# Expert products: the passes with the crossed tokens of two chunks placed behind the other passes of both

## The chip, the core and the metric

The kernel runs on one core of a Trainium2 chip. The metric is the device time of one execution in microseconds (us). Times are medians of several executions; the profile is of one execution, with its own time. The engines are named as in the profile: PE (matmuls), PEld (the loading of PE's stationary operand), DVE (vector), ACT (scalar), POOL (GpSimd) and SP, which issues most DMAs.

## The reference, cut to what matters

There are 32 images of 64 x 1024. Each of two layers runs them through a chain of four small convolutions whose weights depend on a style vector, and then through a feed-forward part that is added to the input. The first feed-forward part has 64 experts of rank 16, of which each token takes 16; the second is one 1024 x 1024 product with 4-bit weights.

```python
def ffn0(x, A, B, Wr):                  # the part that the change touches
    scores = xf @ Wr.T                                   # 2048 tokens x 64 experts
    top_vals, top_idx = top_k(scores, 16)
    G = zeros.at[..., top_idx].set(softmax(top_vals))
    h = einsum('nd,krd->nkr', xf, A)                     # 2048 x (64 * 16)
    return einsum('nkr,kdr->nd', h * G[:, :, None], B) * 2.0

x = x + ffn0(cond0(x, style), A, B, Wr)
x = x + ffn1(cond1(x, style), qweight, scales, zeros, bias)
```

## The kernel before, in words

The images are taken in 16 pairs p, a pair being 128 tokens of 1024 features. There are three stages.

The first stage, `layer0(p)` with what is called around it, makes h. For each pair the loop that begins at line 899 computes the convolutions of later pairs (`begin`: the matmuls of lines 546, 551 and 459; `later`: line 571, called r after the tile that it writes, one call for each of the pair's two images; `weights`: line 480, tile f; `turn`: the transposes of line 621) and, between them, the products of this pair's tokens with the router and the A matrices. These have 64 + 1024 columns and are made in three chunks: c0 with 352 columns, c1 and c2 with 368 each. `layer0` is a generator that yields after each chunk; the loop runs the first chunk, then `later(k + 1, 0)`, the second chunk, then `later(k + 1, 1)` and `weights(k + 2)`, the third chunk, and then the transposes for the next pair.

A product of two fp32 numbers is made of three passes (limbs) in a faster number format. The tokens are split into a high part `th` and a rest `tl` (`split`, lines 589 to 593; the rest is scaled by ACT in line 597), and POOL makes the crossed tokens `td` as their difference in `crossed` (line 605, called at the end of a repetition, after `turn`). The weights are split in the same way into three limbs (`split_weights`, lines 287 to 299; the third limb, which the crossed tokens meet, is made by DVE in line 296 from the other two). The passes with `th` and `tl` add up in one PSUM bank and the passes with `td` in a second one. A pass is 8 matmuls, one for each 128 features. `joined` puts both banks together: ACT reads the first (line 680), DVE the second (line 681). After c0 DVE also finds the 16 best experts (`gates`, lines 685 to 703, with an exponential on ACT in line 698), and POOL multiplies h by the gates at the end (line 709), from where it is stored to `hgd` (line 723). The pairs 0 and 1 (`WHOLE`) are not split: they have one pass of full fp32 matmuls and no crossed tokens.

The second stage, `layer0b(p)`, multiplies h by the B matrices in two chunks of 512 columns, with the same three passes and again no split for the pairs 0 and 1. The rows of h are loaded (line 727) and turned for pair p + 1 (line 739, tile ht) ahead of the products of pair p (tile o). Its `joined` (lines 775 and 776) adds the rows of x, loaded in line 764 into a single region, and the sum is stored to `x1d` (line 798). During the first of these pairs DVE, ACT and POOL also split the B matrices (lines 143, 294, 295, 296) and, from pair 2 to 6, prepare the second layer's convolutions step by step (`factors`, for instance lines 193, 196, 207 and 210). The last pair takes its passes in another order: feature block outermost (`outer=True`).

The third stage, from about 691 us, makes the second layer (`layer1`); its products are written by its own code (line 819).

PSUM is shared out in pools of banks: `cps` has three, for r, the transposes and the c matmuls; `mps` has one, for f and g; `fps` has four, for the products. The buffers `rt` and `ru` of `rest` are single.

The instructions of each engine run in one order, which is fixed when the program is built. The order follows the source in the main, but not in every place: where the builder finds an instruction not yet ready, it can place a later one of the same engine ahead. The semaphore waits are set by it too.

The helper that writes the products is this:

```python
        if outer:
            ...
        else:
            for banks, cols in chunks:
                for l in limbs:
                    for k in range(NC):
                        go(k, l, banks, cols)
```

It is called with one chunk at a time (lines 715 and 795), so each chunk has its passes th, tl, td one after the other, directly followed by its `joined`.

Of the kernel before, what the change touches and what calls it, by code (L numbers as in the profile page):

```python
# [24 lines left out]
NC = L // P  # L25
H = 512
E = 64
R = 16
# [9 lines left out]
CHUNKS = ((0, 18), (18, 41), (41, 64))  # L38
# [23 lines left out]
def adaln_ffn_kernel(ctx: ExitStack, tc: tile.TileContext, t, out: bass.AP):  # L62
    nc = tc.nc
# [19 lines left out]
    def fpst(name):  # L83
        return fps.tile([P, H], F32, tag="fps", name=name)
# [47 lines left out]
    def tokens(tag, name, dt=F32R):  # L132

        return tok.tile([P, NC, P], dt, tag=tag, name=name)
# [464 lines left out]
    toks = {}  # L599
# [37 lines left out]

        return k ^ 1

    def products(chunks, key, ws, order, outer=False):  # L640


        limbs = range(len(toks[key]))

        def go(k, l, banks, cols):
            ps = banks[l == 2]
            w = ws[order(k)]
            if len(limbs) > 1:
                w = w[:, l]
            nc.tensor.matmul(  # L650
                ps,
                toks[key][l][:, k],
                w[:, cols],
                start=(k == 0 and l != 1),
                stop=(k == NC - 1 and l == min(2 * (l // 2) + 1, len(limbs) - 1)),
            )

        if outer:
            for k in range(NC):
                for banks, cols in chunks:  # L660
                    for l in limbs:
                        go(k, l, banks, cols)
        else:
            for banks, cols in chunks:
                for l in limbs:
                    for k in range(NC):
                        go(k, l, banks, cols)

    def layer0(p, ws):

        hs = wk.tile([P, AW], F32, tag="w4", name=f"hs{p}", bufs=3)
        key = f"x0_{p}"
        whole = p in WHOLE

        def joined(col, w, qd):
            dst = hs[:, col : col + w]
            if whole:
                nc.scalar.copy(dst, qd[0])
                return
            nc.scalar.activation(dst, qd[0], AF.Copy, scale=1.0 + 1.0 / RADIX)  # L680
            nc.vector.scalar_tensor_tensor(dst, qd[1], -1.0 / RADIX, dst, ALU.mult, ALU.add)  # L681

        ga = tiny.tile([P, E], F32, tag="ga", name=f"ga_{p}")

        def gates():
            s0 = hs[:, :E]
            m0 = tiny.tile([P, 8], F32, tag="m0", name=f"m0_{p}")
            m1 = tiny.tile([P, 8], F32, tag="m1", name=f"m1_{p}")
            s1 = tiny.tile([P, E], F32, tag="s1", name=f"s1_{p}")
            s2 = tiny.tile([P, E], F32, tag="s2", name=f"s2_{p}")  # L690
            nc.vector.max(m0, s0)
            nc.vector.match_replace(s1, m0, s0, LOW)
            nc.vector.max(m1, s1)
            nc.vector.match_replace(s2, m1, s1, LOW)
            nm = tiny.tile([P, 1], F32, tag="nm", name=f"nm_{p}")
            nc.vector.tensor_scalar_mul(nm, m0[:, 0:1], -1.0)
            ex = tiny.tile([P, E], F32, tag="ex", name=f"ex_{p}")
            nc.scalar.activation(ex, s0, AF.Exp, bias=nm)
            su = tiny.tile([P, 1], F32, tag="su", name=f"su_{p}")
            nc.vector.scalar_tensor_tensor(ga, s2, LOW, ex, ALU.is_equal, ALU.mult)  # L700
            nc.vector.reduce_sum(su, ga, axis=AX.X)
            nc.vector.reciprocal(su, su)
            nc.vector.tensor_scalar_mul(ga, ga, su)

        def gated(c):
            a, b = CHUNKS[c]
            v = hs[:, E + a * R : E + b * R].rearrange("p (e r) -> p e r", r=R)
            g = ga[:, a:b].unsqueeze(2).to_broadcast([P, b - a, R])
            nc.gpsimd.tensor_tensor(v, v, g, ALU.mult)  # L709

        col = 0
        for c, (a, b) in enumerate(CHUNKS):
            w = (b - a) * R + (E if c == 0 else 0)
            qd = [fpst(f"h{p}_{c}_{j}")[:, :w] for j in range(1 if whole else 2)]
            products([(qd, slice(col, col + w))], key, ws, at)
            joined(col, w, qd)
            if c == 0:
                gates()
            col += w
            yield  # L720
        for c in range(3):
            gated(c)
        nc.sync.dma_start(hgd[p], hs[:, E:])
# [30 lines left out]
    def layer0b(p, ws):  # L754

        whole = p in WHOLE
        key = f"h{p}"
        if whole:
            xres = tokens("tl", f"xres{p}", F32).rearrange("p a b -> p (a b)")
        elif p < NP - 1:  # L760
            xres = cv[:, O_Y + 2 * Y : O_Y + 2 * Y + L]
        else:
            xres = wk.tile([P, L], F32, tag="w4", name="xres", bufs=3)
        nc.sync.dma_start(xres, t["x"][p])
        x1 = wk.tile([P, L], F32, tag="w4", name=f"x1_{p}", bufs=3)
        x4 = x1.rearrange("p (f j) -> p j f", f=4)

        def banks(c):
            return [fpst(f"o{p}_{c}_{j}") for j in range(1 if whole else 2)]

        def joined(c, qd):
            cs = slice(c * H, (c + 1) * H)
            v = xres[:, cs]
            if not whole:
                nc.vector.scalar_tensor_tensor(v, qd[1], -SCALING / RADIX, v, ALU.mult, ALU.add)  # L775
            nc.vector.scalar_tensor_tensor(
                x4[:, c * P : (c + 1) * P],
                qd[0].rearrange("p (j f) -> p j f", f=4),
                SCALING if whole else SCALING * (1.0 + 1.0 / RADIX),
                v.rearrange("p (j f) -> p j f", f=4),  # L780
                ALU.mult,
                ALU.add,
            )

        cols = [slice(c * H, (c + 1) * H) for c in range(2)]
        if p == NP - 1:
            qds = [banks(c) for c in range(2)]
            products(list(zip(qds, cols)), key, ws, lambda k: k, outer=True)
            yield
            for c in range(2):  # L790
                joined(c, qds[c])
        else:
            for c in range(2):
                qd = banks(c)
                products([(qd, cols[c])], key, ws, lambda k: k)
                joined(c, qd)
                yield
        nc.sync.dma_start(x1d[p].rearrange("p f j -> p (f j)"), x1)
        v = x1.rearrange("p (f j) -> p j f", f=4)
        for s, js in enumerate((slice(0, 2), slice(L // 4 - 2, L // 4))):  # L800
            nc.gpsimd.tensor_copy(xg[:, p, s].rearrange("p (j f) -> p j f", f=4), v[:, js])
# [97 lines left out]
    for k in range(NP):  # L899
# [4 lines left out]
        if ahead:  # L904
            load(k + 3)
            for h in range(2):
                later(k + 1, h)
            weights(k + 2)
        main = layer0(k, araw if k in WHOLE else wa)
        next(main)  # L910
        if k == 0:
# [31 lines left out]
    for p in range(NP):  # L943
# [4 lines left out]
        if p == NP - 1:  # L948
            clear_y((2, 3))
            begin(NP + 1)  # L950
        main = layer0b(p, braw if p in WHOLE else wb)
        next(main)
        if p in WHOLE:
# [88 lines left out]
```

## Time and profile before

| what | value |
|---|---|
| median of three runs | 1026.52 us (1018.68, 1026.52, 1026.8) |
| profiled execution, its own time | 1025.0 us |
| span in the profile | 1023.2 us |
| mean granted clock of PE | 0.982 |
| PE busy | 958.0 us in 5046 instructions |
| DVE, POOL, ACT busy | 617.5, 462.6, 371.5 us |

The span runs from the first to the last instruction of the program; the execution's own time is 1.8 us longer. The profile's rows show the line of the source, the engine, the tiles written and read (out<-in), the shape, and the number of instructions. In a list of waits the three numbers are the sum in us, the number of waits and the longest one. In a timeline the first two numbers are start and length in us, and a bracket shows how long the engine had been idle and what ended that. An fp32 matmul appears as two records, one of a split pass as one. Since matmuls are pipelined, a record's length is larger than the step from one start to the next.

### The profile page before, as it was taken

The page shows a single profiled execution, that of the slowest core. Times are in us where ns is not written, and L with a number is a line of the kernel's source. Part 1 is how long each engine was busy: PE and PEld are TensorE (multiplying, and loading weights), DVE is VectorE, ACT ScalarE, POOL GpSimd, SP SyncE. Part 2 cuts the span into 40 slices and gives each one's busy share as a digit, 9 for nine tenths or more (in the row PEclk, how much of TensorE's full clock was granted, in tenths as well). Part 3 has the DMA queues.
Part 4 walks back from the last instruction along what each step waited for, and adds up shares of the span by engine and source line. Part 5 has one row for each costly group of instructions (what it writes and reads, how often), then busy time and mean ns, then how long its engine had stood idle before and what let it go on. Part 6 is the DMA issues. An engine that isn't in the chain of part 4 may idle for free.

```text
span 1023.2 us, 14297 instructions
## 1 busy us (share of the span) xinstructions
PE 958.0 (94%) x5046; PEld 842.8 (82%) x5046; DVE 617.5 (60%) x1153; ACT 371.5 (36%) x697; POOL 462.6 (45%) x748
## 2 busy tenths in 40 slices
PE   4789899999999999989889999999899999999997
PEld 4566689999999999885578887888899999999987
DVE  4586465555555555346874444476667776777654
ACT  4255344444444443323331111253333433433331
POOL 4375644444444444435822223225555545555544
PEclk9899899999999999999999999999999999999999
DMA  8323022222222222143333433243111221222111
GB/s 248 86 62 83 20 56 69 63 63 62 62 62 63 62 64 76 67 145 113 107 133 131 139 127 123 83 139 130 62 63 62 92 95 62 76 82 92 42 62 42
DMA packets 40823, 88.84 MB, mean 87 GB/s; under 512 B 13104, under 2 KB 21552, under 8 KB 40752
## 3 DMA queue, kind: packets, MB, share of 16 engines
q1 hardware_dynamic: 39792, 86.94, 26.9%
q10 hardware_dynamic: 960, 0.99, 0.3%
q8 instruction: 40, 0.66, 0.3%
q14 instruction: 31, 0.25, 0.1%
HBM read 62.74 MB, written 25.17 MB: 86 GB/s over the span
## 4 chain that ended last, share of the span: by engine, by line
PE 45%; DVE 4%; ACT 2%; issue 2%; POOL 2%; DMA 1%; POOLq 0%; SPq 0%; DVEq 0%; ACTq 0%
PE o L650 15%; PE q L819 12%; PE r L571 8%; PE f L480 4%; PE c L551 3%; PE h L650 1%; PE ht L739 1%; DVE h L143 1%; DMA cv<-in_x_dram 1%; ACT yt L548 1%; DVE sc L833 1%; PE c L546 1%; ACT wq L347 1%; DMA xb<-x1d 1%; POOL wb L294 0%
## 5 line engine op out<-in xcount | busy, mean ns | idle before, releaser
L571 PE MATMUL r<-cv 128*128 128x256 f32 (+1 forms) x768 | 178.5, 381 | 2.9 <-ACT rt L584 1.5
L571 PEld LDWEIGHTS r<-cv 128*128 128x128 f32 x768 | 142.7, 190 | 23.4 <-ACT rt L584 2.3
L584 ACT ACTIVATE rt<-r,cst,al 128x256 f32<-128x256 f32 x128 | 72.2, 564 | 181.0 <-PE r L571 143.4
L585 DVE TENSOR_TENSOR rs<-rt,ru 128x256 f32<-128x256 f32 x64 | 43.6, 681 | 98.9 <-ACT rt L584 54.8
L480 PEld LDWEIGHTS f<-gs,w1b 128*128 128x128 f32 x576 | 87.1, 193 | 3.1 <-ACT gs L468 1.1
L480 PE MATMUL f<-gs,w1b 128*128 128x192 f32 (+1 forms) x576 | 87.8, 307 | 0.6 <-ACT gs L468 0.6
L551 PE MATMUL c<-cv,c 128*128 128x257 f32 (+1 forms) x256 | 74.1, 410 | 14.0 <-ACT yt L548 5.5
L495 POOL TENSOR_TENSOR cv<-cv 128x256 f32<-128x256 f32 x64 | 49.1, 768 | 74.6 <-DVE cv L493 65.7
L819 PE MATMUL q<-wq,thx 128*128 128x342 f32 x384 | 79.8, 344 | 1.6 <-ACT thx L593 1.6
L493 DVE COPY cv<-f 64x448 f32<-64x448 f32 x64 | 39.9, 623 | 63.1 <-ACT cv L492 62.8
L650 PE MATMUL h<-wa,thx 128*128 128x352 f32 (+1 forms) x336 | 73.1, 353 | 2.8 <-ACT thx L593 2.8
L709 POOL TENSOR_TENSOR hs<-hs,ga 128x368 f32<-128x368 f32 (+1 forms) x48 | 42.3, 882 | 68.6 <-DVE hs L681 56.7
L580 POOL TENSOR_TENSOR ru<-rt 128x256 f32<-128x256 f32 x64 | 41.6, 649 | 69.2 <-ACT rt L579 69.0
L551 PEld LDWEIGHTS c<-cv,c 128*128 128x128 f32 x256 | 46.4, 196 | 32.0 <-ACT yt L548 16.5
L650 PE MATMUL h<-wa,tdx 128*128 128x352 f32 (+1 forms) x336 | 63.6, 331 | 5.8 <-POOL cv L553 4.5
L819 PE MATMUL q<-wq,tlx 128*128 128x342 f32 x384 | 68.9, 322 | 0.0
L681 DVE SCALAR_TENSOR_TENSOR hs<-h,hs 128x368 f32<-128x368 f32 (+1 forms) x42 | 22.5, 535 | 76.9 <-PE h L650 67.1
L834 POOL TENSOR_TENSOR o<-o,sc 128x342 f32<-128x342 f32 (+1 forms) x48 | 41.9, 873 | 59.1 <-DVE o L831 50.4
L492 ACT COPY cv<-f 64x448 f32<-64x448 f32 x64 | 33.8, 529 | 88.5 <-PE f L480 65.3
L819 PEld LDWEIGHTS q<-wq,thx 128*128 128x128 f32 x384 | 62.7, 189 | 3.8 <-ACT thx L593 1.7
L650 PEld LDWEIGHTS h<-wa,tdx 128*128 128x128 f32 x336 | 55.8, 188 | 9.3 <-POOL cv L553 7.4
L650 PE MATMUL o<-wb,thh 128*128 128x512 f32 x224 | 62.8, 411 | 0.4 <-DVE cv L775 0.4
(250 smaller groups left out, 1997.2 us busy)
## 6 DMA issues: line engine op xcount, KB each, us to landing
cv<-in_x_dram SPq DMA_DIRECT2D x64, 256.0 KB, 4.0
hgd<-hs SPq DMA_DIRECT2D x16, 512.0 KB, 2.6
hg<-hgd SPq DMA_DIRECT2D x16, 512.0 KB, 3.5
x1d<-x SPq DMA_DIRECT2D x16, 512.0 KB, 2.9
cv<-x1d SPq DMA_DIRECT2D x128, 64.0 KB, 2.3
xb<-x1d SPq DMA_DIRECT2D x16, 512.0 KB, 3.3
out_dram<-o SPq DMA_DIRECT2D x16, 512.0 KB, 2.6
cv<-in_x_dram SPq DMA_DIRECT2D x13, 512.0 KB, 4.2
```

The source lines that it names most:

```text
L480: nc.tensor.matmul(ps[:, j * C : (j + rhs.shape[1]) * C].rearrange("p (a b) -> p a b", b=C), w1b[:, NB - 1 - q], rhs, start=(n == 0), stop ...
L493: nc.vector.tensor_copy(f[C:, : NT * C], ps[hs, : NT * C])
L495: nc.gpsimd.tensor_tensor(f[:, 4 * P :].rearrange("p (a b) -> p a b", b=P), v[:, :, 0], v[:, :, 1], ALU.add)
L551: nc.tensor.matmul(ps, c0[:, q], xe[:, q, :w_], start=True, stop=True)
L571: nc.tensor.matmul(ps, f[:, k * P : (k + 1) * P], y[:, q, j : j + n_], start=(j == 0), stop=(j == 1),)
L580: nc.gpsimd.tensor_tensor(u, m[:, 0, :w_], m[:, 1, :w_], ALU.add)
L584: nc.scalar.activation(m[:, q, :n_], ps, AF.Identity, bias=b, scale=a)
L585: done["DVE"] = nc.vector.tensor_tensor(r[:, 0], m[:, 2, :w_], u, ALU.subtract)
L650: nc.tensor.matmul(ps, toks[key][l][:, k], w[:, cols], start=(k == 0 and l != 1), stop=(k == NC - 1 and l == min(2 * (l // 2) + 1, len(lim ...
L709: nc.gpsimd.tensor_tensor(v, v, g, ALU.mult)
L819: nc.tensor.matmul(ps, half[:, k], wq[at(k)][:, c * QC : (c + 1) * QC], start=(k == 0 and j == 0), stop=(k == NC - 1 and j == 1),)
L834: nc.gpsimd.tensor_tensor(o[:, cs], o[:, cs], s, ALU.add)
```

## The change

`products` becomes `product`, which writes the passes of one chunk for the limbs that it is given: `Q` stands for the passes with the high and the low tokens, `D` for those with the crossed ones. In `layer0` the Q passes of the chunks 0 and 1 are written first, then the D passes and `joined` of chunk 0, and, after the first yield, the D passes and `joined` of chunk 1. Chunk 2 is as before. The first yield, behind which the loop places `later(k + 1, 0)`, thus comes after 40 matmuls instead of 24, and there are 8 instead of 24 between it and the second yield. In `layer0b` the Q passes of both chunks come first, then D and `joined` of chunk 0, a yield, D and `joined` of chunk 1, and a yield. The last pair keeps its order. For the pairs 0 and 1, which have a single pass, Q is that pass and D is empty. Two chunks now have open sums at the same time, so that all four banks of `fps` are held at once.

```diff
-    def products(chunks, key, ws, order, outer=False):
...
+    def product(chunk, key, ws, order, limbs, ks=range(NC)):
+        banks, cols = chunk
+        n = len(toks[key])
+        for l in limbs:
+            if l < n:
+                for k in ks:
+                    w = ws[order(k)]
+                    if n > 1:
+                        w = w[:, l]
+                    nc.tensor.matmul(
+                        banks[l == 2],
+                        toks[key][l][:, k],
+                        w[:, cols],
+                        start=(k == 0 and l != 1),
+                        stop=(k == NC - 1 and l in (2, min(n, 2) - 1)),
+                    )
+
+    Q, D = (0, 1), (2,)
...
-        col = 0
-        for c, (a, b) in enumerate(CHUNKS):
-            w = (b - a) * R + (E if c == 0 else 0)
-            qd = [fpst(f"h{p}_{c}_{j}")[:, :w] for j in range(1 if whole else 2)]
-            products([(qd, slice(col, col + w))], key, ws, at)
-            joined(col, w, qd)
+        def done_with(c, ch):
+            product(ch, key, ws, at, D)
+            joined(ch[1].start, ch[1].stop - ch[1].start, ch[0])
+
+        two = []
+        for c in range(2):
+            two.append(chunk(c))
+            product(two[c], key, ws, at, Q)
+        for c in range(2):
+            done_with(c, two[c])
             if c == 0:
                 gates()
-            col += w
             yield
+        ch = chunk(2)
+        product(ch, key, ws, at, Q)
+        done_with(2, ch)
+        yield
...
-            for c in range(2):
-                qd = banks(c)
-                products([(qd, cols[c])], key, ws, lambda k: k)
-                joined(c, qd)
+            qds = [banks(c) for c in range(2)]
+            for ch in zip(qds, cols):
+                product(ch, key, ws, lambda k: k, Q)
+            for c, ch in enumerate(zip(qds, cols)):
+                product(ch, key, ws, lambda k: k, D)
+                joined(c, qds[c])
                 yield
```

The new local function `chunk(c)` gives the banks and the columns of a chunk as the removed lines did.

More of the change, by code (lines that the diff above doesn't have):

```diff
@@ L638, in at @@
         return k ^ 1
-    def products(chunks, key, ws, order, outer=False):
[L643 to L667, printed above, removed]
+    def product(chunk, key, ws, order, limbs, ks=range(NC)):
[15 more added lines that the diff above has]
+    Q, D = (0, 1), (2,)
     def layer0(p, ws):
@@ L709, in gated, with chunk @@
             nc.gpsimd.tensor_tensor(v, v, g, ALU.mult)
-        col = 0
-        for c, (a, b) in enumerate(CHUNKS):
+        def chunk(c):
+            a, b = CHUNKS[c]
             w = (b - a) * R + (E if c == 0 else 0)
-            qd = [fpst(f"h{p}_{c}_{j}")[:, :w] for j in range(1 if whole else 2)]
-            products([(qd, slice(col, col + w))], key, ws, at)
-            joined(col, w, qd)
+            col = a * R + (E if c > 0 else 0)
+            banks = [fpst(f"h{p}_{c}_{j}")[:, :w] for j in range(1 if whole else 2)]
+            return banks, slice(col, col + w)
+        def done_with(c, ch):
[7 more added lines that the diff above has]
+            done_with(c, two[c])
             if c == 0:
                 gates()
-            col += w
             yield
+        ch = chunk(2)
+        product(ch, key, ws, at, Q)
+        done_with(2, ch)
+        yield
         for c in range(3):
@@ L787, in layer0b @@
             qds = [banks(c) for c in range(2)]
-            products(list(zip(qds, cols)), key, ws, lambda k: k, outer=True)
+            for k in range(NC):
+                for ch in zip(qds, cols):
+                    product(ch, key, ws, lambda k: k, Q + D, (k,))
             yield
@@ L792, in layer0b @@
         else:
-            for c in range(2):
-                qd = banks(c)
-                products([(qd, cols[c])], key, ws, lambda k: k)
-                joined(c, qd)
+            qds = [banks(c) for c in range(2)]
+            for ch in zip(qds, cols):
+                product(ch, key, ws, lambda k: k, Q)
+            for c, ch in enumerate(zip(qds, cols)):
+                product(ch, key, ws, lambda k: k, D)
+                joined(c, qds[c])
                 yield
```

## The prediction

> **What bounds the kernel now.** I read the page's first part, then the waits of the engines by stage, then timelines around the lines the change touches, and last the table of windows for the clock. The page first:
>
> ```profile
> span 1023.2 us, 14297 instructions
> PE 958.0 (94%) x5046; PEld 842.8 (82%) x5046; DVE 617.5 (60%) x1153; ACT 371.5 (36%) x697; POOL 462.6 (45%) x748
> ```
>
> PE is the bound almost everywhere; a reordering that leaves the 5046 matmuls as they are can only win from PE's idle time. The change touches two stages: layer0 (about 60 to 465 us) and layer0b (466 to 691). From 691 on nothing changes. The waits of PE and of its weight loads in 130 to 465 us (total, times, longest):
>
> ```profile
> PE h L650 <- POOL cv L553: 4.5, 10, 0.5
> PE h L650 <- POOL tdx L605: 1.4, 2, 0.9
> PEld h L650 <- POOL cv L553: 7.4, 10, 0.8
> PEld h L650 <- POOL tdx L605: 2.0, 2, 1.2
> ```
>
> Line 553 is a 0.09 us memset right behind line 605 in POOL's queue, so all twelve are waits for the crossed tokens. One repetition with the wait (around 206) beside the one without (p = 2, around 140), from PE's and POOL's timelines (start, length):
>
> ```profile
> 139.51 1.45 PE L650 MATMUL h<-wa,tlx 128*128 128x352 f32 x8
> 140.79 1.45 PE L650 MATMUL h<-wa,tdx 128*128 128x352 f32 x8
> 142.08 1.49 PE L650 MATMUL h<-wa,thx 128*128 128x368 f32 x8
> ...
> 205.73 2.76 POOL L605 TENSOR_TENSOR tdx<-thx,tlx 128x1024 fp32r<-128x1024 f32 x1 [1.10 <-ACT tlx L597]
> ...
> 206.66 1.45 PE L650 MATMUL h<-wa,tlx 128*128 128x352 f32 x8
> 208.55 1.55 PE L650 MATMUL h<-wa,tdx 128*128 128x352 f32 x8 [0.44 <-POOL cv L553]
> 209.93 2.76 PE L571 MATMUL r<-cv 128*128 128x256 f32 x12
> ```
>
> Undisturbed, 16 passes take 142.08 - 139.51 = 2.57 us (0.16 each); here 209.93 - 206.66 = 3.27 us, 0.70 us more. The crossed tokens are done at 208.49, PE wants them at about 207.95.
>
> **Layer0, part by part.** Nothing is removed or added: same passes, same weights loaded, same evacuations, no DMA added. In a split repetition PE's order goes from c0 (24), r, c1 (24), r, f, c2 (24) to c0 high and low (16), c1 high and low (16), c0 crossed (8), r, c1 crossed (8), r, f, c2. Between the last low pass of c0 and its crossed pass there now lie 16 passes of 368 columns, 2 x 1.33 = 2.7 us (8 take 190.02 - 188.64 = 1.38 at most). Ready 0.5 to 0.6 us late before, the tokens are then ready some 2 us early, and the wait goes.
>
> How large is it? PE's idle gives 4.5 + 1.4 = 5.9, its loads 7.4 + 2.0 = 9.4. [...] By starts: ten repetitions of 0.69 to 0.79 (3.26 to 3.36 less 2.57), 7.1; p = 14, 434.63 - 431.30 - 2.57 = 0.76; p = 15, 454.27 - 450.43 - 2.57 = 1.27. Sum **9.1 us**. I take this; [...] the matmul row is too small, because a busy matmul here overlaps its successor.
>
> What is moved later: r of the first image starts as before right behind c0's crossed passes; only r of the second image comes closer to it, 2.6 + 1.35 = 3.95 us behind instead of 6.6 (216.53 - 209.93). It needs the three PSUM banks that ACT empties:
>
> ```profile
> 211.08 0.56 ACT L584 ACTIVATE rt<-r,cst,al 128x256 f32<-128x256 f32 x1 [2.47 <-PE r L571]
> 211.54 0.34 ACT L698 ACTIVATE ex<-hs,nm 128x64 f32<-128x64 f32 x1
> 211.86 0.48 ACT L579 ACTIVATE rt<-r,al 128x257 f32<-128x257 f32 x1
> 212.73 0.56 ACT L584 ACTIVATE rt<-r,cst,al 128x256 f32<-128x256 f32 x1 [0.39 <-PE r L571]
> ```
>
> They are free 1.7, 2.4 and 3.4 us after r's start, and wanted at 3.95, 4.8 and 5.7: 2.2 us of cover. The buffer rt is single: its next writer waits for DVE's line 585 (213.40 + 0.60, 4.1 after r's start) and is wanted at about 5.0. The second r's results go to the transposes behind c2, still 2.6 + 4.0 us of PE work later. The evacuation of c0 (line 681, 0.54) and the gates (2.4 us on DVE) move with c0's crossed pass; DVE is idle 60.6 us in 150 to 440 in front of line 681 alone, so they cost nothing. SP's loads and store wait for ACT, DVE and POOL, not for these passes. For p = 0 and 1 there are no crossed passes; c1 just moves ahead of r (5.1 us of c1), and ACT and the weight splitting, not PE's order, set the pace at 75 to 82 us: between a 1 us gain and a 1 us loss; I take 0, since ACT's table load and exponential at 77.3 to 78.9 hold rt either way.
>
> **Layer0b.** From p = 5 to 11 PE runs without a gap, 10.9 us per 48 passes: nothing to win. p = 15 keeps its order. What can move is p = 2 and 3:
>
> ```profile
> 504.91 0.80 PE L650 MATMUL o<-wb,tdh 128*128 128x512 f32 x1 [3.91 <-DVE wb L296]
> 505.51 3.30 PE L650 MATMUL o<-wb,thh 128*128 128x512 f32 x8
> ...
> 505.86 0.33 SPq L798 DMA_DIRECT2D x1d<-x  x1
> 508.52 0.33 SPq L727 DMA_DIRECT2D hg<-hgd  x1
> ...
> 524.11 1.05 PE L210 MATMUL dps<-cv 128*128 128x32 f32 x8 [2.15 <-DVE cv L207]
> ...
> 504.90:508.30 3.40, 3.39 (x8) 2.71 (x9) 3.40 (x6) 1.28 (x3) 1.60 (x14) 0.50 0.45 174
> 525.40:528.80 3.40, 3.40 (x10) 2.62 (x9) 1.98 (x9) 2.26 (x6) 0.00 (x0) 0.50 0.24 58
> ```
>
> (In the last two, the windows table, 0.50 is the granted clock.) At p = 2 the last crossed pass waits 3.9 us for its third weight limb. In the new order the 16 passes of c1 (16 x 0.227 = 3.6 us, from 8 in 1.81) lie in front of the crossed ones, so this wait goes nearly whole: PE is through p = 2 at about 507 instead of 512.3. But what is late next is the transposes for p = 4: their rows (line 727) are loaded at 508.52, behind the store of line 798 at 505.86, which waits for DVE, not for PE; with the page's 3.5 us to land they come at 512.0. So PE waits there instead: 0.3 us won. If the order built for PE puts p = 3's passes ahead of these transposes, up to 5 us.
>
> At p = 3, dps waits 2.15 us: line 207 stands on DVE behind line 775, which waits for its x rows (from 518.39, landing at 522.96). In the new order the first evacuation comes behind 40 passes instead of 24, and its rows are there by then. I count this wait as gone, 2.15. The clock: [...] the trace shows 0.50 behind it, and the 8 low passes take 528.65 - 525.31 = 3.34 us instead of 1.82: 1.5 more. [...] by the row 3.65; the row decides. Against it: the new 5 us wait at 507 brings one half-clock stretch (7 passes x 0.2 = 1.4, as behind the old one, which is then saved), and p = 3 may start up to 1 us later for a PSUM bank. 0.3 + 3.65 - 1, less a line 207 that may be late again (0 to 3), and less a second half-clock stretch (0 to 1.5) or with the pull ahead: between a loss of 2 and a gain of 5; I take **2 us**, nearer to the dps row.
>
> **Sum.** 9.1 + 2 = 11. Against the profiled execution (1025.0, span 1023.2): 1014.0. The runs shown have a median of 1026.52, 1.5 above: **1015.5 us**, 1.07% less. A measurement of this kernel tells about 1% from no change (its three runs are 0.8% apart).
>
> **Rivals.**
> - The late stage only moves: layer0 gives its 9.1, but layer0b gives nothing or loses 2, the wait at 507 to 512 and its half clock replacing the old. 1017.5 to 1019.5. For it: the store-and-load chain on SP. 25%.
> - More: p = 3's passes run ahead of the late transposes (4 to 5 us), one more half-clock stretch spared (1.5). 1007 to 1012.5. PE's order does show such pulls: one thx pass at 203.89 stands among the line 546 and 551 matmuls. 15%.
> - The change does not do what it says: the order on PE is not the source's alone, and r can be pulled ahead (four at 427.28), so the crossed pass again follows its low pass closely, or as much is lost elsewhere. 1022 to 1030. Against it: c1's passes need only tokens that are there. 9%.
> - Slower: ACT becomes late. If its line 584 for the first r stood behind the evacuation of c1 and the gates, the second r would find no bank. The cover is 2.2 us; each microsecond beyond costs 1 x 13 repetitions. To end 1% slower (1037) it must eat 11 and add 10.3: 21.3 / 13 = 1.6 stall, so ACT 3.8 us late each time. ACT is 36% busy and waits for PE there. About 1037 to 1045. 6%.
> - The case forecast, 1013 to 1017.5: 45%.
>
> **Numbers.** Faster by over 1% (below 1016.25): the 15% and about 0.75 of the 45%, near 0.49. Slower: 0.06. Rest 0.45. The range leaves out the last two rivals: 1007 to 1022.
>
> **What would show it.** Right: no PE wait at the h passes for POOL; the period of layer0 at 24.5 instead of 25.2 us; crossed passes of c0 directly in front of the first r; dps without its 2 us. Wrong: r waiting for ACT line 584 on PE; an idle stretch before ht at 507 longer than 5 us; PE stalls for line 775 in p = 3 to 14, where c0 and c1 now hold all four banks at once; a layer0 gain under 6.

## The result and the profile after

| what | before | after |
|---|---|---|
| median of 20 runs, alternating | 1024.50 us (1018.68 to 1027.38) | 1019.93 us (1016.34 to 1023.98) |
| ratio after / before | | 0.9962, 95% interval 0.9948 to 0.9976 |
| span of the profiled execution | 1023.2 us | 1018.4 us |
| mean granted clock of PE | 0.982 | 0.977 |

The change is worth 4.6 us, 0.38%. 1015.5 was forecast, a gain of 11 us. The time lies inside the range that was given, but 6.5 us of that gain are missing. First the page of the changed kernel:

```profile
span 1018.4 us, 14300 instructions
PE 956.7 (94%) x5046; PEld 844.0 (83%) x5046; DVE 618.7 (61%) x1153; ACT 371.7 (36%) x697; POOL 463.0 (45%) x748
```

The work is the same to the last matmul, so the difference is idle time and clock. Cut at marks that both traces have (the first transposes t of a pair, the first transposes ht), the span falls into these pieces, in us. "Pairs 0 and 1" runs from the first t behind the start to the third, the piece called layer0 from the fourth t to the first ht (pairs 3 to 15); the 33.7 us between them, the repetition of pair 2, are the same in all traces and are left out.

| piece | before | after | difference |
|---|---|---|---|
| start, to 54.8 / 56.0 | 54.8 | 56.0 | +1.2 |
| pairs 0 and 1 (not split) | 61.6 | 66.4 | +4.8 |
| layer0, pairs 3 to 15 | 312.1 | 302.3 | -9.8 |
| layer0b | 236.8 | 237.1 | +0.3 |
| third stage | 324.2 | 322.9 | -1.3 |

So layer0 gave what was forecast, half of it was lost again in the two pairs ahead of it, and layer0b gave nothing.

**Layer0.** No wait of the h passes for POOL is left in 130 to 465 us. What remains there for h is this (total, times, longest):

```profile
PEld h L651 <- ACT thx L593: 3.6, 2, 1.9
PE h L651 <- ACT thx L593: 3.2, 2, 1.7
```

The repetition shown before, PE's timeline and then POOL's (the product's matmul is now line 651):

```profile
211.12 1.45 PE L651 MATMUL h<-wa,tlx 128*128 128x352 f32 x8
212.41 1.49 PE L651 MATMUL h<-wa,thx 128*128 128x368 f32 x8
213.74 1.48 PE L651 MATMUL h<-wa,tlx 128*128 128x368 f32 x8
215.06 1.44 PE L651 MATMUL h<-wa,tdx 128*128 128x352 f32 x8
216.34 2.76 PE L571 MATMUL r<-cv 128*128 128x256 f32 x12
218.75 1.68 PE L651 MATMUL h<-wa,tdx 128*128 128x368 f32 x8
```

```profile
210.19 2.76 POOL L605 TENSOR_TENSOR tdx<-thx,tlx 128x1024 fp32r<-128x1024 f32 x1 [1.11 <-ACT tlx L597]
```

The crossed tokens are done at 212.95 and wanted at 215.06: 2.1 us early, where they were half a microsecond late. The period of a repetition is 24.4 us.

**Pairs 0 and 1.** PE's timeline in pair 0, of the kernel before and then of the changed one:

```profile
72.68 5.11 PE L650 MATMUL h<-araw,thx 128*128 128x368 f32 x16
77.63 1.03 PE L571 MATMUL r<-cv 128*128 128x256 f32 x4
80.06 2.00 PE L571 MATMUL r<-cv 128*128 128x257 f32 x8 [1.40 <-ACT rt L579]
```

```profile
76.69 2.76 PE L571 MATMUL r<-cv 128*128 128x256 f32 x12
83.70 4.38 PE L571 MATMUL r<-cv 128*128 128x256 f32 x12 [4.26 <-ACT rt L584]
```

ACT's timeline at the same place, again before and after (between the two lines of before lie its table load at 77.33, the exponential and two casts):

```profile
74.72 0.56 ACT L584 ACTIVATE rt<-r,cst,al 128x256 f32<-128x256 f32 x1
...
79.54 0.47 ACT L579 ACTIVATE rt<-r,al 128x257 f32<-128x257 f32 x1
```

```profile
78.75 1.28 ACT L690 ACT_TABLE_LOAD   x1 [2.51 <-DVE nm L688]
80.04 0.35 ACT L690 ACTIVATE ex<-hs,nm 128x64 f32<-128x64 f32 x1
80.29 0.75 ACT L295 CAST wa<-wah 128x64 fp32r<-128x64 f32 x2
80.95 0.46 ACT L670 COPY hs<-h 128x368 f32<-128x368 f32 x1
82.42 0.76 ACT L295 CAST wa<-wah 128x512 fp32r<-128x512 f32 x2 [1.02 <-DVE wah L143]
83.09 0.56 ACT L584 ACTIVATE rt<-r,cst,al 128x256 f32<-128x256 f32 x1
```

The first image's r is finished at 79.4. ACT empties its bank only at 83.09, behind the table load, the exponential and two groups of casts for the splitting of A, the last of which waits for DVE itself. In the kernel before, the first r had begun at 70.08 and ACT emptied its first bank at 74.72, ahead of the table load; only the other two banks came behind it. So c1 in front of r does two things: r misses that early place in ACT's queue, and c1 no longer stands between the two r. The second r follows the first directly on PE now and waits 4.26 us (before: 1.40). Its 12 matmuls then take 4.38 us where the same 12 take 2.76 undisturbed: the granted clock is 0.50 from 83.4 to 86.8 us.

**Layer0b.** PE and DVE of the changed kernel at pairs 2 and 3:

```profile
501.52 2.00 PE L651 MATMUL o<-wb,tdh 128*128 128x512 f32 x8
503.95 2.11 PE L651 MATMUL o<-wb,tdh 128*128 128x512 f32 x8 [0.42 <-DVE x L782]
505.90 1.03 PE L745 MATMUL ht<-ident,hg 128*128 128x128 f32 x8
513.27 3.75 PE L651 MATMUL o<-wb,thh 128*128 128x512 f32 x8 [6.34 <-DVE cv L781]
...
526.93 0.97 PE L210 MATMUL dps<-cv 128*128 128x32 f32 x8
```

```profile
506.79 5.74 DVE L269 TENSOR_TENSOR cv<-cv 128x256 f32<-128x256 f32 x6
512.44 0.68 DVE L781 SCALAR_TENSOR_TENSOR cv<-o,cv 128x512 f32<-128x512 f32 x1
```

Both old waits are gone: 3.91 us for the third limb, 2.15 us in front of dps. In their place stands one of 6.34 us. It isn't the transposes: ht runs at 505.90 without a wait. Pair 3 wants the PSUM banks of pair 2, whose evacuation (line 781) is at 512.44 on DVE, behind 5.74 us of line 269, a step of `factors`. The queue was already like that in the kernel before, on DVE:

```profile
508.73 4.27 DVE L269 TENSOR_TENSOR cv<-cv 128x256 f32<-128x256 f32 x4
512.92 0.69 DVE L775 SCALAR_TENSOR_TENSOR cv<-o,cv 128x512 f32<-128x512 f32 x1
```

Its PE came to pair 3 at about 513.3, since the third limb had held it up, and waited only 0.42 us for line 775. The old wait hid the new one.

**The clock.** Three half-clock stretches of the changed kernel in the windows table (columns: stretch, length, busy time with number of instructions of PE, PEld, DVE, ACT, POOL, granted clock, DMA share, GB/s):

```profile
83.40:86.80 3.40, 3.10 (x7) 2.51 (x8) 3.40 (x4) 1.07 (x3) 3.40 (x5) 0.50 0.00 0
462.30:465.70 3.40, 3.40 (x7) 1.34 (x6) 2.24 (x4) 2.03 (x4) 3.04 (x3) 0.50 0.36 143
510.10:516.90 6.80, 3.63 (x9) 2.92 (x10) 6.66 (x11) 1.96 (x3) 0.59 (x4) 0.50 0.00 0
```

Each begins during a wait or right behind it: 4.26, 1.93 and 6.34 us.

### The profile page after: what moved, and what is told of

The parts are those of the page before. It is cut to its first block, busy times and chain, and to the rows that moved or that the text cites. A ratio compares the mean times of both kernels' runs of the same rounds, so it can differ in the third digit from the quotient of the medians.

```text
span 1018.4 us, 14300 instructions
## 1 busy us (share of the span) xinstructions
PE 956.7 (94%) x5046; PEld 844.0 (83%) x5046; DVE 618.7 (61%) x1153; ACT 371.7 (36%) x697; POOL 463.0 (45%) x748
## 4 chain that ended last, share of the span: by engine, by line
PE 77%; DVE 8%; POOL 4%; ACT 4%; issue 4%; DMA 2%; SPq 0%; POOLq 0%; DVEq 0%; ACTq 0%
PE h L651 17%; PE r L571 15%; PE o L651 15%; PE q L829 12%; PE f L480 7%; PE c L551 6%; DVE h L143 2%; PE c L546 2%; POOL wa L294 2%; ACT thx L593 1%; ACT yt L548 1%; PE ht L745 1%; DMA cv<-in_x_dram 1%; PE g L459 1%; DVE sc L843 1%
## 5 line engine op out<-in xcount | busy, mean ns | idle before, releaser
L651 PE MATMUL h<-wa,thx 128*128 128x352 f32 (+1 forms) x336 | 70.7, 345 | 3.2 <-ACT thx L593 3.2
L651 PE MATMUL o<-wb,thh 128*128 128x512 f32 x224 | 61.7, 406 | 6.6 <-DVE cv L781 6.3
L552 DVE SCALAR_TENSOR_TENSOR cv<-c,al,yt 128x257 f32<-128x257 f32 (+1 forms) x128 | 57.1, 479 | 12.3 <-PE c L551 5.4
L492 ACT COPY cv<-f 64x448 f32<-64x448 f32 x64 | 33.9, 529 | 81.2 <-PE f L480 61.0
L829 PEld LDWEIGHTS q<-wq,tlx 128*128 128x128 f32 x384 | 62.5, 191 | 0.0
```

The lines of the kernel that those rows point to most:

```text
L552: nc.vector.scalar_tensor_tensor(d, ps, a, yt[:, :w_], ALU.mult, ALU.add)
L651: nc.tensor.matmul(banks[l == 2], toks[key][l][:, k], w[:, cols], start=(k == 0 and l != 1), stop=(k == NC - 1 and l in (2, min(n, 2) - 1)),)
L829: nc.tensor.matmul(ps, half[:, k], wq[at(k)][:, c * QC : (c + 1) * QC], start=(k == 0 and j == 0), stop=(k == NC - 1 and j == 1),)
```

## The experiments

The theory after the traces: the order in layer0 gives about 10 us; the new order of the unsplit pairs 0 and 1 costs about 5, by ACT's queue; in layer0b DVE's queue takes back what the third limb gives. The rival: the parts depend on each other, so that undoing one only shifts the loss; or chance in the clock explains half the gap.

Medians and ratios are against the kernel before, run beside each (medians there 1024.4 to 1025.5). The last four columns are pieces of the profiled spans, cut as above.

| kernel | us | ratio, 95% interval | start | pairs 0, 1 | layer0 (3 to 15) | layer0b |
|---|---|---|---|---|---|---|
| e1 whole_old | 1012.58 | 0.9877 (0.9853 to 0.9900) | 52.5 | 61.7 | 302.2 | 237.1 |
| e2 layer0_split | 1014.17 | 0.9888 (0.9866 to 0.9911) | 55.9 | 62.2 | 302.2 | 235.9 |
| e3 layer0b_only | 1024.18 | 0.9992 (0.9978 to 1.0007) | 52.7 | 61.7 | 312.1 | 236.2 |
| e4 set1_behind | 1006.10 | 0.9811 (0.9789 to 0.9834) | 54.0 | 61.8 | 302.2 | 227.3 |
| e5 split_parts | 1018.07 | 0.9936 (0.9912 to 0.9960) | 53.9 | 66.9 | 302.2 | 235.7 |
| e6 td2_after | 1036.75 | 1.0110 (1.0072 to 1.0148) | 56.3 | 66.9 | 311.3 | 243.3 |
| e7 td2_before | 1090.80 | 1.0641 (1.0596 to 1.0686) | 55.4 | 62.6 | 370.9 | 240.6 |
| e10 set1_layer0 | 1010.18 | 0.9854 (0.9822 to 0.9886) | 55.6 | 62.0 | 302.3 | 231.2 |
| e11 new_split_behind | 1010.16 | 0.9855 (0.9826 to 0.9884) | 55.6 | 65.1 | 302.3 | 227.3 |
| e12 old_split_behind | 1009.29 | 0.9848 (0.9822 to 0.9875) | 54.5 | 63.5 | 302.2 | 229.0 |

**Undoing pairs 0 and 1 (e1).**

```diff
             two.append(chunk(c))
             product(two[c], key, ws, at, Q)
-        for c in range(2):
+            if whole:
+                done_with(c, two[c])
+                if c == 0:
+                    gates()
+                yield
+        for c in range(0 if whole else 2):
```

> The changed kernel, but pairs 0 and 1 of layer0 (which have no crossed passes) keep the old order c0, r, c1, r. Theory A: moving c1 ahead of r at pair 0 costs the 4.8 us that the first repetition became longer (34.6 to 39.4 us between the transposes), so this gives 1019.9 - 4.8 = 1015 us, ratio to before 0.991, and the 4.3 us wait of r for ACT line 584 near 80 us is 1.4 us again. Rival B: the start differs by chance (clock windows, DMA), then it stays at 1019 to 1021 and the wait stays or goes without effect on the end.

Measured 1012.58, and 61.7 us for the two pairs instead of 66.4. PE's timeline in pair 0 has c1 between the two r again:

```profile
70.34 5.11 PE L651 MATMUL h<-araw,thx 128*128 128x368 f32 x16
75.28 1.03 PE L571 MATMUL r<-cv 128*128 128x256 f32 x4
77.84 2.00 PE L571 MATMUL r<-cv 128*128 128x257 f32 x8 [1.53 <-ACT rt L579]
```

Part of rt is late here too, but PE has 5.1 us of c1 to do meanwhile. The median is 7.3 us below the changed kernel. The profiled executions place 4.7 of that in these pairs; 3.5 lie in the start, whose code is the same (see the end), so I count 4.7 for the order.

**Only layer0's split pairs (e2), only layer0b (e3).** e2 is e1 with layer0b's old order; e3 has layer0's old order and layer0b's new one.

> Only the split pairs 2 to 15 of layer0 in the new order; pairs 0 and 1 and all of layer0b as before. Theory A: the twelve waits for the crossed tokens are worth 9.8 us between the transposes of pair 2 and the end of layer0, and layer0b's new order about nothing: 1024.5 - 9.8 = 1014.7, ratio 0.990, the same as the run with only pairs 0 and 1 in the old order within 2 us. Rival C: layer0b's new order is worth the 2 us that were forecast, then this one is 2 us slower than that run, about 1017.

> Only layer0b in the new order, layer0 as before. Theory A: the 4.4 us won at pair 2 (the wait for the third weight limb) come back as a wait of 6 us of pair 3's first passes for DVE's evacuation of pair 2, with the half clock behind it, and 3.7 us at the prepared matmuls of the second layer are won: sum between -1 and +1, 1023.5 to 1025.5, ratio 0.999 to 1.001. Rival C: 1022.5 or less, ratio 0.998, no wait for DVE at pair 3.

Measured 1014.17 and 1024.18. Layer0's new order alone takes 9.9 us out of layer0, the same as with the rest of the change: the parts don't depend on each other. Layer0b's new order alone is not to be told from nothing (ratio 0.9992); its trace has the wait of 6.3 us at pair 3 already, so layer0's order doesn't cause it.

**The steps of `factors` behind the evacuation (e4).** e1 with two lines; `done["joined"]` is the last instruction of `joined` on DVE:

```diff
         if 1 < p < 7:
-            next(set1, None)
+            with tc.issue_after(done["joined"].ins):
+                next(set1, None)
```

> As the run with pairs 0 and 1 in the old order, and the steps that prepare the second layer (lines 183 to 283, pairs 2 to 6 of layer0b) are put behind the last evacuation written before them, on DVE, so that line 269's six additions (5.7 us) no longer stand in front of pair 2's evacuation. Theory A (DVE's order holds the PSUM bank): the 6.3 us wait at pair 3 goes, with its half clock (1.6): 5 to 7 us below that run, about 1009. Rival D (the bank is held by something else, or the DVE time is only shifted to a later wait): within 2 us of that run.

Measured 1006.10, 6.5 us below e1 in the median. PE and DVE at the same place:

```profile
497.51 1.03 PE L750 MATMUL ht<-ident,hg 128*128 128x128 f32 x8
498.58 2.09 PE L651 MATMUL o<-wb,thh 128*128 128x512 f32 x8
```

```profile
497.76 0.67 DVE L786 SCALAR_TENSOR_TENSOR cv<-o,cv 128x512 f32<-128x512 f32 x1
498.47 1.10 DVE L787 SCALAR_TENSOR_TENSOR x<-o,cv 128x512 f32<-128x512 f32 x1
```

The evacuation has no line 269 in front of it, pair 3 starts right behind the transposes, and the 6.34 us are gone with what followed them: pair 3's first eight passes take 2.09 us here, 3.75 in the changed kernel at half clock. Layer0b takes 227.3 us instead of 237.1. The wait (6.3 in e1 too) and the slower passes make 8.0 of these 9.8 us, if e1's passes took as long as the changed kernel's; what the other 1.8 are was not shown. That DVE's queue, and no load and no transpose, held the bank is shown. This is the fastest kernel of the study.

**The same with layer0b's old order (e10).** Only the order in layer0b differs from e4.

> Only pairs 2 to 15 of layer0 in the new order, layer0b in the old order, and the steps of factors at pairs 2 to 6 placed behind the evacuation of the products. Beside the best version so far (1006.1), which differs only by the new order in layer0b. Theory (layer0b's new order takes away the 3.9 us wait for the third limb, and it is the DVE queue that took this back): with the queue mended both are worth their own, so this run is 3 to 5 us longer than that version, 1009 to 1011, with the wait for line 296 of 3 to 4 us still there. Rival (mending the queue alone is the whole gain, the third limb would be early too, since DVE's line 269 no longer stands around it): within 1 us of 1006.

Measured 1010.18, 4.1 us above e4, and in its layer0b on PE

```profile
496.42 0.65 PE L651 MATMUL o<-wb,tdh 128*128 128x512 f32 x1 [3.88 <-DVE wb L296]
```

is the old wait. So layer0b's new order is worth 3.9 us of the stage (231.2 less 227.3), once DVE's queue doesn't take them back.

**The crossed tokens twice.** In both kernels `crossed` computes its result twice in a row on POOL, 2.76 us more each time; nothing else is edited.

```diff
+            nc.gpsimd.tensor_tensor(
+                *(v.rearrange("p a b -> p (a b)") for v in (td, *toks[key])), ALU.subtract
+            )
             nc.gpsimd.tensor_tensor(
```

> The changed kernel with the crossed tokens computed twice in a row on POOL (2.8 us more each time), everything else the same. Theory (the change works by putting 2.7 us of passes in front of the crossed ones; the tokens are then about 2 us early): 2.8 - 2 = 0.8 us of wait in each of twelve repetitions of layer0, period 24.4 to about 25.2, time 5 to 15 us longer than the changed kernel. Rival (the waits went because POOL itself is earlier or the tokens are not what is waited for): no more than 2 us longer, period as it was. If the cover were used up already, 33 us longer.

> The kernel before with the crossed tokens computed twice in a row on POOL, as in the run beside it. Theory: no cover is left here, so all of the 2.8 us shows in each of twelve repetitions: period 25.2 to about 28, 12 x 2.8 = 33 us longer than the kernel before (25 to 40, since PE may place a few of the next convolutions' matmuls into the gap), and about 25 us longer than the changed kernel with the same doubling. Rival (the builder fills the gap with other matmuls): under 15 us longer.

In the changed kernel layer0 grows by 9.0 us (311.3 less 302.3), the period from 24.4 to 25.1. 2.76 us of delay less 2.1 of cover leaves 0.66 a repetition, and the waits (total, times, longest) are back:

```profile
PEld h L654 <- POOL cv L553: 7.1, 10, 0.8
```

The whole is 16.8 us slower, a little more than expected, since 6.2 us come in layer0b, where POOL makes these tokens too (PE's longest wait for the evacuation on DVE is 8.4 there instead of 6.3; how the one leads to the other was not traced). In the kernel before, layer0 grows by 58.8 us, far more than the 33 of the delay. PE's timeline, its waits in layer0 and the windows table there:

```profile
249.43 1.44 PE L653 MATMUL h<-wa,tlx 128*128 128x352 f32 x8
253.88 2.71 PE L653 MATMUL h<-wa,tdx 128*128 128x352 f32 x8 [3.01 <-POOL cv L553]
```

```profile
PE h L653 <- POOL cv L553: 31.9, 11, 3.0
PE h L653 <- POOL tdx L608: 4.7, 2, 2.5
```

```profile
222.60:229.40 6.80, 6.16 (x17) 5.43 (x18) 3.58 (x14) 0.80 (x2) 0.71 (x3) 0.50 0.29 77
```

The waits are 36.6 us, 30.7 more than the 5.9 of before. The other 28 us of the 58.8 fit what the half clock costs. In the stretch shown the granted clock is 0.50; in the kernel before it is 1.00 from 129.5 to 504.9 us. The mean over e7's span of 1086.2 us is 0.953, against 0.982 over 1023.2 us before. If all that is missing was at half clock, that is 102 and 37 us of it, 65 more. With PE busy for 6.16 of 6.80 us, as in the stretch shown, that is 59 us of work, and half of it, about 30 us, would be saved at full clock; this is an estimate from these numbers. My expectation left the clock out.

**ACT's queue in pair 0 (e5).** The changed kernel with its whole order; A is split for pair 0 in two parts, the second written behind `later(1, 0)`, so that ACT has rt ahead of the last six casts.

```diff
-                split_weights(araw, AW, range(5), wa, "wa")
+                split_weights(araw, AW, range(3), wa, "wa")
...
             later(k + 1, 0)
+        if k == 0:
+            with tc.issue_after(done["DVE"].ins), tc.issue_after(done["POOL"].ins):
+                split_weights(araw, AW, range(3, 5), wa, "wa")
```

> The changed kernel with all of its order, pairs 0 and 1 included; only the splitting of the A matrices for pair 0 is written in two parts, so that on ACT the evacuations of r (line 584, three of them) stand ahead of the last six casts of line 295 and not behind them. Theory (the wait of 4.3 us for r's bank in pair 0 comes from ACT's queue, where rt stands behind two casts, the table load and the exponential, and c1 no longer covers that): the wait falls under 2 us, pair 0 takes 35 to 36 us instead of 39.4, the time is 4 to 7 us under the changed kernel, about 1014. Rival (r simply has too little PE work in front of it, whatever ACT does): the wait stays above 3 us and the time within 2 us of the changed kernel. Second rival: the casts are late instead, and PE waits for limbs of A in pair 1: no gain, with a new wait on line 651 for ACT or DVE.

Measured 1018.07: no gain that counts. The wait for rt is gone, as the theory said: ACT empties the first bank at 76.18, right behind the exponential. So the splitting, on ACT and in front of the gates on DVE, had held r, and not the table load and the exponential by themselves. Pair 0 takes 33.1 us (53.9 to 87.0) instead of 39.4. But pair 1 takes 33.8 instead of 27.0. PE's timeline shows where it went:

```profile
89.48 0.66 PE L621 MATMUL t<-ident,rs 128*128 128x128 f32 x4 [1.92 <-POOL rs L586]
...
92.83 2.08 PE L551 MATMUL c<-cv,c 128*128 128x257 f32 x4 [2.25 <-ACT thx L630]
```

The two r now run together (24 matmuls from 74.17, without a wait), but the second image's results go through ACT, POOL (lines 580, 581, 586) and DVE behind the second part of the splitting, and the transposes want them at 87.6. The wait was moved one step down, which none of my three expectations had.

**The splitting behind both images' r (e11, e12).** In both, the second part of the splitting is written behind `later(1, 1)`, and `factors` stands as in e4. e11 has the changed order in pairs 0 and 1, e12 the old one.

> The changed kernel with all of its order, pairs 0 and 1 included, with the steps of factors placed behind the evacuation in layer0b, and with the last two blocks of A split behind the evacuations of both images' r in pair 0 (instead of in front of them). Theory (the new order of pairs 0 and 1 costs something only because the splitting stands in the queues of ACT, DVE and POOL between r and its results, and c1 no longer covers it): the waits of 4.3 us for r's bank and of 1.9 us for the turned rows go, the pairs 0 and 1 together take 62 to 63 us instead of 66.4 to 66.9, and the time is within 3 us of the best version, 1006. Rival (c1 in front of r costs its 5 us wherever the splitting stands): 66 us or more, 1010 to 1014.

> The best version so far (old order for pairs 0 and 1, new order elsewhere, the steps of factors behind the evacuation), with the last two blocks of A split behind the evacuations of both images' r in pair 0. Theory: with c1 between the two r there is cover enough and only the wait of 1.5 us at r in pair 0 can go: pairs 0 and 1 in 60 to 62 us instead of 61.8, time 1004.5 to 1007. Rival (the splitting then comes too late for pair 2 or holds the convolutions' evacuations): 63 us or more, over 1008.

Measured 1010.16 and 1009.29, with 65.1 and 63.5 us for the two pairs: in e11 the pairs lie between theory and rival and the time in the rival's range, in e12 the rival came. (e12's layer0b is 1.7 us longer than e11's, with the same order there; why was not shown.) In e11 the waits for rt and rs are gone; PE now waits for the tokens of the next convolutions, and ACT shows why:

```profile
93.21 1.95 PE L551 MATMUL c<-cv,c 128*128 128x257 f32 x4 [2.70 <-ACT thx L630]
```

```profile
90.86 0.76 ACT L295 CAST wa<-wah 128x512 fp32r<-128x512 f32 x2 [2.10 <-DVE wah L143]
91.64 0.53 ACT L492 COPY cv<-f 64x448 f32<-64x448 f32 x1
92.20 0.47 ACT L670 COPY hs<-h 128x368 f32<-128x368 f32 x1
92.56 1.08 ACT L630 COPY thx<-t 128x512 f32<-128x512 f32 x2
```

A cast that waits 2.10 us for DVE stands in front of them. With the splitting in its old place the new order costs 4.7 us (66.4 less 61.7); with it behind both r, 1.6 (65.1 less 63.5). So two thirds of the cost depend on where the splitting stands in the queues; what the last 1.6 us are was not found out. None of the three runs that moved the splitting beat the old order with the splitting in its old place (e4); other places were not tried.

## Why the prediction was wrong, point by point

- **Layer0, 9.1 us: right.** 9.8 in the changed kernel, 9.9 in e1, e2 and e4. Idle time of the weight loads (9.4) and the instructions' starts (9.1) measured it well, idle time of the matmuls (5.9) did not. The cover of "some 2 us" is 2.1, and e6 used it up as computed. The rival that ACT becomes late did not come in these pairs.
- **Pairs 0 and 1, "I take 0": the step that failed.** It said that "ACT's table load and exponential at 77.3 to 78.9 hold rt either way", and bounded the loss by 1 us. Neither half of this held. Before, ACT had emptied the first bank of r at 74.72, ahead of the table load; with c1 moved in front, r came too late for that, and all of rt waited until 83.09 behind the table load and the casts, of which e5 shows that the splitting is what counts. And c1, 5.1 us, had been PE's work in the meantime. The wait of 1.40 us became 4.26, 2.9 more; the half clock behind it cost 4.38 less 2.76, 1.6 more: 4.5 of the measured 4.8. How much each of the two effects took was not measured apart. In the split pairs I had worked out just this cover (2.2 us left); here I did not.
- **Layer0b, 2 us: wrong in the wait, and in its size.** The gains were read rightly (third limb, dps). I gave the third limb's back to the transposes, "their rows (line 727) are loaded at 508.52"; that load was for pair 5 (the one for pair 4 is at 486.69 in the trace of before), and ht ran at 505.90 in the changed kernel. The bank that I priced at "up to 1 us" is the one that held, 6.3 us, for line 269 in front of the evacuation on DVE, which the trace of before shows in front of line 775. The stage came out at +0.3, each of the two executions having one more half-clock stretch behind a wait of about 2 us (before at 638.0, after at 462.3).
- **The clock: the row was right.** At dps the 2.15 us gap had cost a half-clock stretch (0.50 from 525.4 to 528.8), and it was priced by that. The wait of 1.93 us at 459.9 in the changed kernel brought half clock as well (0.50 from 462.3 to 465.7). In e5 the clock was 0.66 in the mean from 90 to 100 us, behind and between waits of 1.92 and 2.25 us, and four c matmuls took 2.08 us there instead of 1.15.
- **Not in the sum:** the start (+1.2) and the third stage (-1.3). The start has 13.7 us of half clock from 32.2 us on instead of 6.8 from 33.9 on, the third stage one stretch of 3.4 us (at 728.5) instead of two (702.9 and 733.6); so both look like the clock and not the change, which no run tested.
- **Sum.** Forecast 9.1 + 0 + 2 = 11.1; measured 9.8 - 4.8 - 0.3 - 1.2 + 1.3 = 4.8. With the failed step undone, e1, the time is 1012.6, within 3 us of the forecast; that it is so near is in part luck, since layer0b still gave nothing and e1's profiled start is 3.5 us shorter. Of the rivals "the late stage only moves" is nearest (to 1019.5): layer0b did give nothing, with a half-clock wait in place of the old; but its mechanism, the load on SP, is not the one found.

## What to carry to other kernels

When work is moved away from between two instructions, ask what it covered there, also in the stages where another engine sets the pace: "that engine is late either way" doesn't price the step; the time until that engine is done, less the work left on this one, does. Ask also whether the work that now starts later loses its place in the other engine's queue. And when a wait is to go, read the queue of every engine that has to answer next, evacuations above all, up to the time at which the waiting engine will now arrive; a wait of 3.9 us can hide one of 6.3. Independent steps written into such a queue belong behind the evacuation: two lines of source were worth more here (6.5 us) than the change as it stood (4.6).

## What the runs showed of the hardware

Some of PE's waits in the traces of before and after, and the granted clock of the windows table there or behind them (end: start of the matmul that had waited):

| wait, us | kernel, end | granted clock |
|---|---|---|
| 6.34 | after, 513.27 | 0.50 from 510.1 to 516.9 |
| 4.26 | after, 83.70 | 0.50 from 83.4 to 86.8 |
| 3.91 | before, 504.91 | 0.50 from 504.9 to 508.3 |
| 2.15 | before, 524.11 | 0.50 from 525.4 to 528.8 |
| 2.15 | before, 636.94 | 0.50 from 638.0 to 641.4 |
| 2.14 | before, 732.43 | 0.50 from 733.6 to 737.0 |
| 2.13 | after, 634.48 | 1.00 from 516.9 to 728.0 |
| 2.12 | after, 727.65 | 0.50 from 728.5 to 731.9 |
| 1.93 | after, 461.78 | 0.50 from 462.3 to 465.7 |
| 1.75 | before, 465.47 | 1.00 from 462.2 to 469.0 |
| 1.34 and 0.66 | before, 700.97 and 702.81 | 0.50 from 702.9 to 706.3 |
| 1.30 and 0.66 | after, 697.41 and 699.26 | 1.00 from 695.0 to 702.9 |

The length of a wait alone doesn't tell these cases apart: the same instruction (line 429) waited 2.15 us in the one kernel and 2.13 in the other, with half clock behind the first and full clock behind the second. What decides it was not shown. In e7 the waits grew by 30.7 us and the stage by 58.8, so a wait of 2 to 3 us cost about twice its length there.

The 8 fp32 matmuls of an unsplit chunk of 368 columns took 5.11 us (at 72.68 in the kernel before), one split pass of as many columns 1.49 us (at 142.08). A record of 1.45 us at 139.51 is followed by the next start 1.28 us later.

The start, whose code all these kernels share, took between 52.5 and 56.3 us in the profiled executions. The kernel before had 6.8 us of half clock in it (54.8 us in all), the changed one 13.7 (56.0 us). What decides it was not looked into; differences of two or three microseconds between single executions are therefore read from the pieces and not from the spans.
